# Values by whole tiles, four input sums on TensorE, and last halves that read h in place, in a four-layer graph network

## The chip, the cores and the metric

The kernel runs on one core of a Trainium2 chip. A core has five engines that work side by side and wait for each other by semaphores: TensorE (PE in the profile; PEld is its weight load), VectorE (DVE), ScalarE (ACT), GpSimd (POOL) and SyncE (SP, which here only issues DMAs). TensorE reads SBUF and writes PSUM; DVE and ACT read both. The metric is the device time of one execution, in microseconds (us); the runs are summed up by their median. The profiled execution is one more run, and has its own time and its own span, from the first to the last instruction.

## The reference

`x` holds 128 graphs of 64 nodes with 256 features, all fp32. Four layers follow one another, and each adds its graph network to `x` and normalises over the features:

```python
x = _layernorm(x + _L0_gnn_ref(x, adj, ...), axis=-1)
x = _layernorm(x + _L1_gnn_ref(x, adj, adj, ...), axis=-1)
x = _layernorm(x + _L2_gnn_ref(x, adj, ...), axis=-1)
x = _layernorm(x + _L3_gnn_ref(x, adj, ...), axis=-1)
```

Layer 0 aggregates over the graph, applies a two-layer perceptron and normalises both of its stages over all 8192 rows (a batch norm). Layer 1 aggregates, then runs attention with four heads of 64 and a perceptron:

```python
q = (x1 @ Wq).reshape(B, N, H, hd).transpose(0, 2, 1, 3)
v = (x1 @ Wv).reshape(B, N, H, hd).transpose(0, 2, 1, 3)
attn = jax.nn.softmax(scores, axis=-1)
o = jnp.einsum('bhnm,bhmd->bhnd', attn, v)
```

Layer 2 is two graph convolutions and then four LSTMs (p = 1 to 4), each over windows of p nodes; the last state of a window replaces the node at its end. Layer 3 is one graph attention over `h @ W`, with scores from two vectors:

```python
Wh = jnp.einsum('bnf,fo->bno', h, W)
e = s1[:, :, None] + s2[:, None, :]
attention = jax.nn.softmax(e, axis=-1)
h_prime = jnp.einsum('bij,bjo->bio', attention, Wh)
```

## The kernel before

The 8192 rows are cut into 16 blocks of 512 rows: 8 graphs of 64 nodes, laid out as four tiles of 128 rows (two graphs one above the other) by 256 features. `tm` views a buffer of 128x1024 by rows (tile, feature), `fm` by features (two chunks of 128 features, 512 rows). PSUM is used as four buffers of 128x1024 (`PS`); SBUF has eight temporaries of that size and more that become free later (`mem`). All matmuls are fp32.

A recording layer writes the program out in full. Every piece of work is a generator that yields a `step`: the engine, its expected time, how many PSUM buffers (`ps`) and temporaries (`sl`) it takes or gives back, and for TensorE the way the array is divided (`tbl`: whole, "columns" for halves, "quarter"). `flow` (L144) is a planner: it keeps a clock for each engine, takes the step that can start soonest, and so fixes, when the program is built, the order of instructions on each engine. A margin added to the start time is multiplied by a number drawn from `DRAWS`, one seed for each 50 us of planned time, so other seeds give another order everywhere. Where the plan has TensorE idle for over about a microsecond, `keep_awake` (L136) puts filler matmuls of 512 columns (L142) whose result nobody reads.[...]

The places that the change touches:

- `end_block` (L767) ends layer 0 for a block. It loads the block's input (L771), applies the batch norm's scale and shift to H on ACT (L774), transposes it to rows by eight transposes on TensorE (`to_tm`, L376), and adds the input on DVE (L782). Blocks are ended in the order 0, 1, 12, 13, 14, 15, 2, 3 and so on, the first six of them around the first blocks of layer 1. `block` (L789) is layer 1; its layer norms are statistics on DVE (L302 to L304), a power on POOL (L325), one small DVE step (L328) and four ACT steps (L331).
- In `block`, queries and keys are made by `mm_fm` (L382), then the values (L846). The attention's last product needs a head's values on the same partitions as its attention weights, and heads lie in pairs on the two halves of 64 partitions. Before, values are computed in halves of the array: 32 matmuls of 64 output rows by 128 columns, which leaves both halves in place, so one ACT copy of 128x1024 (L856) empties the PSUM buffer.
- The LSTMs of layer 2 keep h transposed in `hT`: features on partitions, and in the free dimension chunk, node and graph, with 32 graphs of a quarter of the batch side by side. Their matmuls are L1113, L1185 and, for the last units of p = 4, L1321 and L1323; their last write of h in such a unit is L1446. `units_of` splits the last quarter's p = 4 in two units of 16 graphs (blocks 12 and 13, and 14 and 15).
- `last_block` (L1513) is layer 3 for a block, or for half of one (two tiles) in the last quarter of the batch, blocks 12 to 15. It loads the rows of `x` that layer 2 left in DRAM (L1518), copies h from `hT` into the order of graphs (ACT, L1524), transposes it (L376), adds half of it to `x` on DVE (L1535; h is kept doubled), normalises, transposes again (L370), copies to SBUF (L1549, L1551), multiplies with W and the score vectors (L1564), makes the scores (L1588, L1589), the softmax (L1593 to L1604), transposes it (L1610), applies it (L1620), adds (L1631), normalises and stores (L1635).

Of the kernel before, what the change touches and what calls it, by code (L numbers as in the profile page):

```python
# [11 lines left out]
ALU = mybir.AluOpType  # L12
# [3 lines left out]
P = 128  # L16
B, N, D = 128, 64, 256
NBLK = 16
TB = 512
NT = 4  # L20
# [8 lines left out]
LAG, LAG_T = 0.06, 0.2  # L29
MARGIN = {"T": 0.5, "V": 0.5, "S": 0.5}  # L30
STRETCH = 50.0
DRAWS = [119, 456, 684, 0, 152, 590, 97, 0, 0, 316, 775, 750, 291, 668, 396, 690, 972, 316, 700, 299, 810, 345, 289, 861, 902, 463, 567, 883, 455, 277, 848, 910, 108, 288, 531, 607, 103, 756, 415, 205, 829, 978, 419, 437, 870, 596, 976, 248, 270, 919]


@with_exitstack
def kernel(ctx: ExitStack, tc: tile.TileContext, a: dict, out: bass.AP):
    nc = tc.nc
    V, S, G, T = nc.vector, nc.scalar, nc.gpsimd, nc.tensor
# [11 lines left out]
    def tm(s):  # L50

        return s.rearrange("p (t d) -> p t d", t=NT)
# [64 lines left out]
    def mark(*key):  # L117
        done[key] = Clock.end
# [7 lines left out]
    def step(e, us, ps=0, sl=0, waits=True, at=None, tbl=None):  # L126

        return (e, us, ps, sl, waits, at, tbl)
# [113 lines left out]
    Xs = [Xp[i // 2][:, i % 2, :] for i in range(NBLK)]  # L248
# [3 lines left out]
    H = [fm(s) for s in Hs]  # L252
    hT = [t.rearrange("p (c n b) -> p c n b", c=2, n=N) for t in Hg]
    XD = [dram.tile([P, NT, D], F32, tag=f"xd{i}", name=f"xd{i}") for i in range(NBLK)]

    PS = Stock([ctile([P, NT * D], f"ps{j}", psp) for j in range(4)])
    mem = Stock([ctile([P, NT * D], f"t{j}", big) for j in range(TEMPS)])
# [15 lines left out]
    halves = slice(0, N), slice(N, P)  # L273
    for s in range(2):
        h = halves[s]
# [8 lines left out]
    ident = ctile([P, P], "ident")  # L284
# [34 lines left out]
    def ln_steps_act(y):  # L319

        n = y.shape[1]
        yield step("V", 0.3 + 0.53 * n)
        mv, rs = stats(y)
        yield step("G", 1.0)
        G.tensor_tensor(rs, rs, neghalf[:, :n], ALU.pow)  # L325
        yield step("V", 0.2, tbl="m")
        nm = sm.tile([P, n], F32, tag="ln_nm", name="ln_nm")
        V.scalar_tensor_tensor(nm, mv[:, :, 0], -1.0, rs, ALU.mult, ALU.mult)  # L328
        yield step("S", 0.1 + 0.5 * n)
        for t in range(n):  # L330
            S.activation(  # L331
                y[:, t, :], y[:, t, :], AF.Identity, scale=rs[:, t : t + 1], bias=nm[:, t : t + 1]
            )
# [38 lines left out]
    def to_tm(ps, yT):  # L372

        for t in range(ps.shape[1]):
            for c in range(2):
                T.transpose(ps[:, t, c * P : (c + 1) * P], yT[:, c, t * P : (t + 1) * P], ident)  # L376
# [13 lines left out]
    def mm_tm(ps, yT, w, nk):  # L390

        for t in range(NT):
            for k in range(nk):
                T.matmul(
                    ps[:, t, :],
                    yT[:, k, t * P : (t + 1) * P],
                    w[:, k, :],
                    start=(k == 0),
                    stop=(k == nk - 1),
                )  # L400
# [22 lines left out]
    with c0:  # L423
# [310 lines left out]
        Wc, Wq, Wk, Wv = (WA[:, j, :].rearrange("p (k m) -> p k m", k=2) for j in range(4))  # L734
# [24 lines left out]
    sc2, sh2, _ = bn["bn2"]  # L759

    Wv_par = Wv.rearrange("p k (u r e) -> p k r u e", u=2, r=2)

    NORMED = range(1)

    def end_block(i):  # L767
        x = X[i]
        yield step("Q", 6.0, sl=1)
        xin = mem.take()  # L770
        nc.sync.dma_start(tm(mem[xin]), x_blk[i])  # L771
        for c in range(2):
            yield step("S", 0.7)
            S.activation(  # L774
                H[i][:, c, :], H[i][:, c, :], AF.Identity, scale=sc2[:, c : c + 1], bias=sh2[:, c : c + 1]
            )
        yield step("T", 0.9, ps=1)
        ps = PS.take()
        to_tm(tm(PS[ps]), H[i])
        mark("h", i)  # L780
        yield step("V", 1.25, ps=-1)
        V.tensor_tensor(x, tm(PS[ps]), tm(mem[xin]), ALU.add)  # L782
        PS.give(ps)
        mem.give(xin)
        if i in NORMED:
            yield from ln_steps_act(x)
        mark("end", i)

    def block(i):  # L789
        x = X[i]  # L790
# [4 lines left out]
        ps = PS.take()  # L795
# [6 lines left out]
        ps = PS.take()  # L802
# [14 lines left out]
        ps = PS.take()  # L817
        s_x1 = mem.take()
        to_fm(fm(PS[ps]), y)
        yield step("S", 1.05, ps=-1)  # L820
        x1T = fm(mem[s_x1])
# [3 lines left out]
        for w in (Wq, Wk):  # L825
            yield step("T", 3.45, ps=1, sl=1)
            ps = PS.take()
# [8 lines left out]
        qT, kT = fm(mem[qk[0]]), fm(mem[qk[1]])  # L836


        yield step("T", 3.6, ps=1, sl=1, tbl="columns")
        ps = PS.take()  # L840
        s_v = mem.take()
        pv = PS[ps].rearrange("p (b u e) -> p b u e", b=8, u=2)
        for b in range(8):
            for r in range(2):
                for k in range(2):
                    T.matmul(  # L846
                        pv[r * N : (r + 1) * N, b, :, :],
                        x1T[:, k, b * N : (b + 1) * N],
                        Wv_par[:, k, r, :, :],
                        start=(k == 0),  # L850
                        stop=(k == 1),
                    )
        mem.give(s_x1)
        yield step("S", 1.05, ps=-1, waits=False)
        v = mem[s_v].rearrange("p (b u e) -> p b u e", b=8, u=2)
        S.copy(mem[s_v], PS[ps])  # L856
        PS.give(ps)

        yield step("G", 2.4, waits=False, tbl="m")
# [4 lines left out]
        ps = PS.take()  # L864
        s_e = mem.take()
        pq = PS[ps].rearrange("p (r g m) -> p r g m", r=2, g=8)
        for t in range(NT):
            for u in range(2):
                for s in range(2):
                    b = 2 * t + s  # L870
                    for r in range(2):
# [4 lines left out]
                            start=True,  # L876
                            stop=True,
# [4 lines left out]
        e = mem[s_e].rearrange("p (g r m) -> p g r m", g=8, r=2)  # L882
# [19 lines left out]
        ps = PS.take()  # L902
# [9 lines left out]
        ps = PS.take()  # L912
        s_o = mem.take()
        po = fm(PS[ps])
        for b in range(8):
            t, s = b // 2, b % 2
            for u in range(2):
                for r in range(2):
# [4 lines left out]
                        start=True,  # L923
                        stop=True,
# [7 lines left out]
        ps = PS.take()  # L932
# [9 lines left out]
        ps = PS.take()  # L942
# [13 lines left out]
        for hf in range(2):  # L956
            yield step("T", 3.45, ps=1, sl=1)
            ps = PS.take()
# [14 lines left out]
        ps = PS.take()  # L973
        for t in range(NT):
            for k in range(4):
# [4 lines left out]
                    start=(k == 0),  # L980
                    stop=(k == 3),
# [82 lines left out]
    def hT_block(i):  # L1064

        return hT[i // 4][:, :, :, (i % 4) * 8 : (i % 4) * 8 + 8]
# [443 lines left out]
        return None if ("ws", p) not in done else max(t, done[("ws", p)])  # L1510


    def last_block(i, t0=0, nt=NT):  # L1513

        yield step("Q", 4.0, sl=1)
        s_x = mem.take()
        x = tm(mem[s_x])[:, :nt, :]
        nc.sync.dma_start(x, XD[i][:, t0 : t0 + nt, :])  # L1518
        r = nt / NT
        yield step("S", 0.2 + 1.9 * r, sl=1)  # L1520
        s_h = mem.take()
# [7 lines left out]
        ps = PS.take()  # L1529
        px = tm(PS[ps])[:, :nt, :]  # L1530
# [5 lines left out]
        PS.give(ps)  # L1536
        yield from ln_steps_act(x)

        yield step("T", 0.9 * r, ps=1, sl=1)
        ps = PS.take()  # L1540
        s_xT = mem.take()
        px = fm(PS[ps])[:, :, : nt * P]
# [11 lines left out]
        for t in range(0, nt, 2):  # L1554
            end = t == nt - 2
            yield step("T", 1.75, ps=1, sl=int(t == 0))
            ps = PS.take()
# [4 lines left out]
            for j in range(2):  # L1562
                for k in range(2):
# [4 lines left out]
                        start=(k == 0),  # L1568
                        stop=(k == 1),
# [13 lines left out]
        e, aT, d = (mem[s_e][:, j * nt * N : (j + 1) * nt * N].rearrange("p (t m) -> p t m", t=nt) for j in range(3))  # L1583
        G.tensor_tensor(d, bc_mid(unit2, nt), bc_last(s12[:, :nt, 1], N), ALU.mult)
        yield step("T", 0.1 + 0.9 * r, ps=1)
        ps = PS.take()
# [19 lines left out]
        ps = PS.take()  # L1606
# [8 lines left out]
        ps = PS.take()  # L1615
        po = PS[ps].rearrange("p (e u d) -> p e u d", e=2, u=2)
        for t in range(0, nt, 2):
            for j in range(2):
                for h in range(2):
# [4 lines left out]
                        start=True,  # L1624
                        stop=True,
# [17 lines left out]
    for i in blocks:  # L1643
        while n < at_end.get(i, NBLK):
            j = ends[n]
# [27 lines left out]
    for g in range(NG - 1):  # L1673
        read = [("read", i) for i in range(4 * g, 4 * g + 4)]
# [53 lines left out]
    def last_of(i, *part):  # L1728
# [17 lines left out]
        start=done["bn2", 0],  # L1746
# [49 lines left out]
```

## Time and profile before

| | |
|---|---|
| median of 3 runs | 2317.06 us (2316.89 to 2318.54) |
| the profiled execution | 2318.26 us, its span 2316.5 us |
| granted TensorE clock, mean | 0.997 |
| TensorE waits by the profile, all over | under 2 us each but for one of 5.5 near the start |
| filler matmuls (L142) | 29 (58 records): 24.9 us, at 0.43 us a record |
| last matmul to the end | 10.1 us |

The page gives the busy time of each engine and its share of the span, then the span in 40 slices with one digit a slice for each engine (9 is 90% or more). The view by stages gives the same in microseconds between two limits, with the granted clock and DMA at its end. The timeline lists instructions of one line together: start, time from the first start to the last end, engine, line, operation, what it writes and reads, shapes, how many records, and in brackets the idle time before it and who ended it. A matmul's end is modelled, so records overlap. The view of one line gives shortest, median and longest duration in nanoseconds for each name it writes and reads.

### The profile page before, as it was taken

To read this page: it belongs to the slowest core of one execution; us is meant where nothing else is said; L and a number is where in the kernel's file an instruction comes from. 1 tells how busy PE (TensorE), PEld (TensorE's weight loads), DVE (VectorE), ACT (ScalarE), POOL (GpSimd) and SP (SyncE) were. 2 spreads that over 40 slices of the span, in tenths; PEclk is the share of its full clock that TensorE was granted. 3 is DMA by queue.
4 is the path that set the end of the run, shared out by engine and by line. 5 is a ranking of instruction groups with operands and counts; after the bars stand their busy time and mean duration, and the time that the engine had idled before them with its cause. 6 is when DMAs were issued, how large, how long until landed. Compare 5 with 4: busy or idle time off the path is not lost. (4 is left out here: it accounts for less than half of the span.)

```text
span 2316.5 us, 40592 instructions
## 1 busy us (share of the span) xinstructions
PE 2270.1 (98%) x16974; PEld 1757.4 (76%) x16974; DVE 1332.9 (58%) x2869; ACT 1176.1 (51%) x2265; POOL 437.1 (19%) x323
## 2 busy tenths in 40 slices
PE   8999999999999999999999999999999999999997
PEld 5558667666666767567667888999999889888884
DVE  5557776767565668437444444454445655664577
ACT  2257556555554545544544343444434644654576
POOL 0012133232322235113220001001100110111012
PEclk9999999999999999999999999999999999999999
DMA  6100411000000000000100000000001000001111
GB/s 173 47 1 1 138 38 33 10 11 10 10 10 10 11 10 19 28 2 28 37 28 19 1 1 1 19 1 1 1 1 37 1 10 28 19 19 37 37 56 55
DMA packets 42632, 57.90 MB, mean 25 GB/s; under 512 B 6224, under 2 KB 35536, under 8 KB 42448
## 3 DMA queue, kind: packets, MB, share of 16 engines
q1 hardware_dynamic: 41344, 54.22, 7.1%
q8 instruction: 133, 2.18, 0.4%
q10 hardware_dynamic: 1104, 1.08, 0.1%
q14 instruction: 51, 0.42, 0.1%
HBM read 38.52 MB, written 16.78 MB: 24 GB/s over the span
## 5 line engine op out<-in xcount | busy, mean ns | idle before, releaser
L325 POOL TENSOR_TENSOR ln_rs<-ln_rs,neghalf 128x4 f32<-128x4 f32 (+1 forms) x104 | 111.8, 1075 | 722.5 <-DVE ln_rs L304 573.0
L1185 PE MATMUL ps<-x,x 128*128 128x256 f32 x832 | 204.5, 379 | 0.0
L1185 PE MATMUL ps<-t,x 128*128 128x256 f32 x736 | 179.0, 380 | 0.8 <-DVE t L1244 0.8
L1081 ACT ACTIVATE x<-ps,bih 128x512 f32<-128x512 f32 (+5 forms) x185 | 95.5, 552 | 150.4 <-PE ps L1113 97.7
L1185 PEld LDWEIGHTS ps<-x,x 128*128 128x128 f32 x832 | 156.0, 190 | 18.7
L1185 PEld LDWEIGHTS ps<-t,x 128*128 128x128 f32 x736 | 138.2, 190 | 20.3 <-DVE t L1244 1.2
L1081 ACT ACTIVATE t<-ps,bih 128x512 f32<-128x512 f32 (+5 forms) x151 | 79.5, 563 | 127.2 <-PE ps L1113 85.0
L331 ACT ACTIVATE x<-x,ln_nm,ln_rs 128x256 f32<-128x256 f32 x212 | 110.2, 593 | 43.8 <-DVE ln_nm L328 43.3
L382 PE MATMUL ps<-t,W1T 128*128 128x512 f32 x256 | 115.3, 595 | 0.0
L1081 ACT ACTIVATE x<-x,bih 128x512 f32<-128x512 f32 (+5 forms) x142 | 72.1, 559 | 44.2 <-DVE x L1251 44.2
L303 DVE BATCH_NORM_AGGREGATE ln_mv<-ln_st 128x2 f32<-128x6 f32 x448 | 81.6, 182 | 15.3
L302 DVE BATCH_NORM_STATS2 ln_st<-x 128x6 f32<-128x256 f32 x224 | 89.7, 401 | 0.3
L1113 PE MATMUL ps<-h,wL 128*128 128x192 f32 (+2 forms) x456 | 89.7, 351 | 0.0
L1113 PE MATMUL ps<-h,x 128*128 128x256 f32 x384 | 86.8, 380 | 0.0
L1113 PE MATMUL ps<-t,wL 128*128 128x512 f32 x192 | 83.9, 593 | 1.2 <-ACT t L909 1.2
L1113 PEld LDWEIGHTS ps<-h,wL 128*128 128x128 f32 x456 | 70.0, 190 | 17.4 <-issue 16.7
L382 PEld LDWEIGHTS ps<-t,W1T 128*128 128x128 f32 x256 | 46.4, 190 | 47.5 <-issue 47.3
L1113 PEld LDWEIGHTS ps<-h,x 128*128 128x128 f32 x384 | 72.8, 190 | 10.4 <-issue 0.5
L1244 DVE COPY x<-ps 128x256 f32<-128x256 f32 (+2 forms) x71 | 26.7, 377 | 86.6 <-PE ps L1185 86.2
L1251 DVE TENSOR_TENSOR x<-ps,x 128x512 f32<-128x512 f32 (+2 forms) x71 | 42.4, 598 | 51.0 <-PE ps L1185 41.0
L331 ACT ACTIVATE t<-t,ln_nm,ln_rs 128x256 f32<-128x256 f32 x104 | 54.1, 592 | 32.1 <-DVE ln_nm L328 32.1
L1113 PEld LDWEIGHTS ps<-t,wL 128*128 128x128 f32 x192 | 36.3, 190 | 44.7 <-issue 42.8
(715 smaller groups left out, 5408.6 us busy)
## 6 DMA issues: line engine op xcount, KB each, us to landing
t<-in_x_dram SPq DMA_DIRECT2D x24, 512.0 KB, 5.5
xd<-x SPq DMA_DIRECT2D x16, 512.0 KB, 2.7
h<-in_x_dram SPq DMA_DIRECT2D x7, 512.0 KB, 4.0
x<-xd SPq DMA_DIRECT2D x6, 512.0 KB, 3.4
out_dram<-x SPq DMA_DIRECT2D x6, 512.0 KB, 2.9
wL<-in_L_gnn_Wih_dram SPq DMA_DIRECT2D x2, 1024.0 KB, 5.0
x<-in_L_gnn_Whh_dram SPq DMA_DIRECT2D x2, 1024.0 KB, 5.2
t<-xd SPq DMA_DIRECT2D x4, 512.0 KB, 4.3
```

Source lines behind the costliest of these rows:

```text
L302: V.bn_stats(st[:, t, :], y[:, t, :])
L303: V.bn_aggr(mv[:, t, :], st[:, t, :])
L325: G.tensor_tensor(rs, rs, neghalf[:, :n], ALU.pow)
L331: S.activation(y[:, t, :], y[:, t, :], AF.Identity, scale=rs[:, t : t + 1], bias=nm[:, t : t + 1])
L382: T.matmul(ps[:, c, :], w[:, k, (off + c) * P : (off + c + 1) * P], yT[:, k, :], start=(k == 0), stop=(k == nk - 1),)
L1081: S.activation(dst, z, AF.Tanh, bias=bl[:, p - 1, 2 * g + c : 2 * g + c + 1], scale=(1.0 if g == 2 else 0.5) * (1.0 if p == 1 else 0.5),)
L1113: T.matmul(spread(fm(PS[ps])[:, j, :n], q), WL[p][0][:, k, m], x_of(0, q)[:, k], start=(k == 0), stop=(k == 1),)
L1185: T.matmul(dst, WS[p][name](k, g), y[:, k], start=first and k == 0, stop=k == 1, skip_group_check=not first)
L1244: V.tensor_copy(y[:, 1, :], v[:, 0, :])
L1251: V.tensor_tensor(y[:, 0:2, :], v[:, 2:4, :], y[:, 0:2, :], ALU.add)
```

## The change

There are three edits and new seeds.

Values are computed by `mm_tm` like the other products: eight matmuls of 128 rows by 256 columns. The pairs of heads then lie in the free dimension, and four ACT copies of 64 partitions by 512 elements bring each half of the rows to the half of the partitions where its head belongs.

For blocks 12 to 15 (`SUM_BY_T`), `end_block` no longer transposes and adds. TensorE multiplies the identity with the input's tile (256 columns, starts the sum) and H's two chunks with the identity (128 columns each, added on top), four times, and ACT copies the sum to SBUF. These are ordinary matmuls, not transposes.

In `last_block`, half blocks read h where it lies: for each tile, graph and chunk one matmul has h of that graph (64 columns, 32 numbers apart) as its stationary operand and the identity as its moving one, in halves of the array. DVE adds the result in two instructions. Whole blocks go on as before, in `sum_of_copies`.

```diff
-DRAWS = [119, 456, 684, 0, 152, 590, ...]
+DRAWS = [555, 824, 612, 0, 95, 823, ...]
...
+    SUM_BY_T = (12,13,14,15)
...
-        yield step("T", 0.9, ps=1)
+        yield step("T", 2.65 if i in SUM_BY_T else 0.9, ps=1)
         ps = PS.take()
-        to_tm(tm(PS[ps]), H[i])
-        mark("h", i)
-        yield step("V", 1.25, ps=-1)
-        V.tensor_tensor(x, tm(PS[ps]), tm(mem[xin]), ALU.add)
+        if i in SUM_BY_T:
+            for t in range(NT):
+                T.matmul(tm(PS[ps])[:, t, :], ident, tm(mem[xin])[:, t, :], start=True, stop=True)
+                for c in range(2):
+                    T.matmul(
+                        tm(PS[ps])[:, t, c * P : (c + 1) * P],
+                        H[i][:, c, t * P : (t + 1) * P],
+                        ident,
+                        start=False,
+                        stop=True,
+                        skip_group_check=True,
+                    )
+            mark("h", i)
+            yield step("S", 1.05, ps=-1)
+            S.copy(Xs[i], PS[ps])
+        else:
+            to_tm(tm(PS[ps]), H[i])
...
-        yield step("T", 3.6, ps=1, sl=1, tbl="columns")
+        yield step("T", 3.45, ps=1, sl=1)
         ps = PS.take()
         s_v = mem.take()
-        pv = PS[ps].rearrange("p (b u e) -> p b u e", b=8, u=2)
-        for b in range(8):
-            for r in range(2):
-                for k in range(2):
-                    T.matmul(
-                        pv[r * N : (r + 1) * N, b, :, :],
-                        x1T[:, k, b * N : (b + 1) * N],
-                        Wv_par[:, k, r, :, :],
...
-        yield step("S", 1.05, ps=-1, waits=False)
-        S.copy(mem[s_v], PS[ps])
+        mm_tm(tm(PS[ps]), x1T, Wv, 2)
+        mem.give(s_x1)
+        pv = PS[ps].rearrange("p (t u r e) -> p t u r e", t=NT, u=2, r=2)
+        v = mem[s_v].rearrange("p (b u e) -> p b u e", b=8, u=2)
+        yield step("S", 2.4, ps=-1, waits=False)
+        for s in range(2):
             for r in range(2):
+                S.copy(v[halves[r], s::2, :, :], pv[halves[s], :, :, r, :])
...
+    def direct_sum(i, t0, nt, x):
+
+        r = nt / NT
+        yield step("T", 1.8 * r, ps=1, tbl="columns")
+        ps = PS.take()
+        px = PS[ps].rearrange("p (e u d) -> p e u d", e=2, u=2)
+        for t in range(nt):
+            for s in range(2):
+                for c in range(2):
+                    T.matmul(
+                        px[halves[s], t % 2, t // 2, c * P : (c + 1) * P],
+                        hT_block(i)[:, c, :, 2 * (t0 + t) + s],
+                        ident,
+                        start=True,
+                        stop=True,
+                    )
+        mark("read", i)
+        yield step("V", 0.1 + 1.2 * r, ps=-1)
+        for j in range(2):
+            V.scalar_tensor_tensor(x[:, j::2, :], px[:, j, : nt // 2, :], 0.5, x[:, j::2, :], ALU.mult, ALU.add)
...
+        if nt < NT:
+            yield from direct_sum(i, t0, nt, x)
+        else:
+            yield from sum_of_copies(i, t0, nt, x)
```

More of the change, by code (lines that the diff above doesn't have):

```diff
@@ L31 @@
 STRETCH = 50.0
-DRAWS = [119, 456, 684, 0, 152, 590, 97, 0, 0, 316, 775, 750, 291, 668, 396, 690, 972, 316, 700, 299, 810, 345, 289, 861, 902, 463, 567, 883, 455, 277, 848, 910, 108, 288, 531, 607, 103, 756, 415, 205, 829, 978, 419, 437, 870, 596, 976, 248, 270, 919]
+DRAWS = [555, 824, 612, 0, 95, 823, 924, 783, 0, 77, 0, 664, 0, 363, 656, 902, 351, 574, 489, 0, 99, 684, 176, 923, 880, 530, 427, 46, 867, 911, 330, 952, 468, 0, 995, 634, 175, 950, 362, 0, 989, 997, 384, 358, 116, 975, 487, 599, 389, 118]
 @with_exitstack
@@ L759 @@
     sc2, sh2, _ = bn["bn2"]
-    Wv_par = Wv.rearrange("p k (u r e) -> p k r u e", u=2, r=2)
     NORMED = range(1)
+    SUM_BY_T = (12,13,14,15)
     def end_block(i):
@@ L776, in end_block @@
             )
-        yield step("T", 0.9, ps=1)
+        yield step("T", 2.65 if i in SUM_BY_T else 0.9, ps=1)
         ps = PS.take()
-        to_tm(tm(PS[ps]), H[i])
-        mark("h", i)
-        yield step("V", 1.25, ps=-1)
-        V.tensor_tensor(x, tm(PS[ps]), tm(mem[xin]), ALU.add)
+        if i in SUM_BY_T:
[15 more added lines that the diff above has]
+            to_tm(tm(PS[ps]), H[i])
+            mark("h", i)
+            yield step("V", 1.25, ps=-1)
+            V.tensor_tensor(x, tm(PS[ps]), tm(mem[xin]), ALU.add)
         PS.give(ps)
@@ L836, in block @@
         qT, kT = fm(mem[qk[0]]), fm(mem[qk[1]])
-        yield step("T", 3.6, ps=1, sl=1, tbl="columns")
+        yield step("T", 3.45, ps=1, sl=1)
         ps = PS.take()
         s_v = mem.take()
-        pv = PS[ps].rearrange("p (b u e) -> p b u e", b=8, u=2)
-        for b in range(8):
-            for r in range(2):
-                for k in range(2):
-                    T.matmul(
-                        pv[r * N : (r + 1) * N, b, :, :],
-                        x1T[:, k, b * N : (b + 1) * N],
-                        Wv_par[:, k, r, :, :],
[L850 to L853, printed above, removed]
-        yield step("S", 1.05, ps=-1, waits=False)
-        v = mem[s_v].rearrange("p (b u e) -> p b u e", b=8, u=2)
-        S.copy(mem[s_v], PS[ps])
+        mm_tm(tm(PS[ps]), x1T, Wv, 2)
[4 more added lines that the diff above has]
+        for s in range(2):
+            for r in range(2):
+                S.copy(v[halves[r], s::2, :, :], pv[halves[s], :, :, r, :])
         PS.give(ps)
@@ L1510, in sums_at, with sum_of_copies @@
         return None if ("ws", p) not in done else max(t, done[("ws", p)])
[L1513 to L1518, printed above, removed]
+    def sum_of_copies(i, t0, nt, x):
         r = nt / NT
@@ L1537, in last_block @@
         yield from ln_steps_act(x)
+    def direct_sum(i, t0, nt, x):
[17 more added lines that the diff above has]
+            V.scalar_tensor_tensor(x[:, j::2, :], px[:, j, : nt // 2, :], 0.5, x[:, j::2, :], ALU.mult, ALU.add)
+        PS.give(ps)
+        yield from ln_steps_act(x)
+    def last_block(i, t0=0, nt=NT):
+        yield step("Q", 4.0, sl=1)
+        s_x = mem.take()
+        x = tm(mem[s_x])[:, :nt, :]
+        nc.sync.dma_start(x, XD[i][:, t0 : t0 + nt, :])
+        r = nt / NT
+        if nt < NT:
+            yield from direct_sum(i, t0, nt, x)
+        else:
+            yield from sum_of_copies(i, t0, nt, x)
         yield step("T", 0.9 * r, ps=1, sl=1)
```

## The prediction, made before the changed kernel ran

> **What bounds the kernel.** I read the busy shares first, then the 40 slices, then the timeline of TensorE where its slices aren't full, and last the stages around the end.
>
> ```profile
> PE 2270.1 (98%) x16974; PEld 1757.4 (76%) x16974; DVE 1332.9 (58%) x2869; ACT 1176.1 (51%) x2265; POOL 437.1 (19%) x323
> PE   8999999999999999999999999999999999999997
> ...
> 300.00:500.00 200.00, 196.63 (x1928) 137.78 (x1926) 130.50 (x269) 111.85 (x162) 64.94 (x38) 1.00 0.07 24
> 2261.00:2316.50 55.50, 39.44 (x304) 26.43 (x302) 40.98 (x154) 36.31 (x105) 11.87 (x17) 0.90 0.17 58
> ```
>
> The last two lines are stages: their limits, their length, then busy time of PE, PEld, DVE, ACT and POOL. TensorE (PE) carries the span: nothing else is over 60%, and only the first and the last slices show room. So I count TensorE's work up to the last product of the LSTM (L1323, ending at 2261), and beyond it a tail of 55.5 us that hangs on latency (clock 0.90 there). Busy time must not be summed: it contains the pipeline's end of each matmul. I take start to start:
>
> ```profile
> 294.00 0.61 PE L1029 MATMUL ps<-bdAT,h 128*128 128x128 f32 x4
> ...
> 311.70 3.40 PE L394 MATMUL ps<-wA,t 128*128 128x256 f32 x15
> 314.94 1.04 PE L905 MATMUL ps<-ident,t 128*128 128x128 f32 x8
> 315.91 3.76 PE L846 MATMUL ps<-wA,t 128*64 128x128 f32 x64
> 319.60 1.16 PE L919 MATMUL ps<-h,t 64*64 64x64 f32 x64
> ```
>
> L394: (3.40 - 0.379)/14 = 0.216 us a record of 256 columns. L905: (1.04 - 0.273)/7 = 0.110 of 128 columns. L846: (3.76 - 0.273)/63 = 0.0553 of 128 columns in half the array. A transpose makes one record (L905: 8 for 8), an ordinary fp32 matmul two (L1029: 4 for 2). Entering the half-array form costs 315.91 - 314.94 - 8 x 0.110 = 0.09, leaving it 319.60 - 315.91 - 64 x 0.0553 = 0.15.
>
> **Values (16 blocks).** Out: 64 records x 0.0553 = 3.54. In: 16 x 0.216 = 3.46. That is -0.08 a block, -1.4 in all. The trace shows what a change of tiling costs, 0.09 and 0.15; the Trainium skill, "TensorEngine Tiling (Array Packing)", section Tiling Modes, says that such a change drains the array, without a time. By the rule, priced from the rows, every Values step saves two drains, 16 x 0.24 = 3.8. But the order of the built program decides: quarter-array neighbours remain, and all changes of form, priced one by one (0.09 into a narrower one, 0.14 to 0.15 out), go from 25.8 to 24.8: -1.0. I take that. Here the evacuation becomes four copies of 64x512 on ACT for one of 1.01. Nearest row: L1549, 128x512 out of PSUM, 0.58; four are 2.0 (overlapped) to 2.3, so +1.2 a block, +19.7 on ACT over 300 to 1150, where it is 53% busy (451 of 850 us). The buffer of PSUM is held that much longer; below nothing it can't go. Queued behind it on ACT are other blocks' copies. Cost taken: 0; the price if the cover fails is the slower rival below.
>
> **Four sums by TensorE (blocks 12 to 15).** Out: 8 transposes, 0.88, and a DVE addition of 1.22. In: 4 x 2 x 0.216 = 1.73 for the input and 8 x 2 x 0.110 = 1.76 for h, as these are no transposes: 3.49, so +2.6 each, +10.4 on TensorE; DVE loses 4.9, ACT gets four copies of 1.01. The matmuls now wait for the input's load instead of DVE. In the trace each of the first eight loads lands by 256.4 and TensorE comes to them after 258, so no stall; queued behind would be all of TensorE. The place has room:
>
> ```profile
> 250.14 7.03 PE L142 MATMUL ps<-ident 128*128 128x512 f32 x16
> 257.00 2.02 PE L376 MATMUL ps<-ident,h 128*128 128x128 f32 x17
> 259.52 1.86 PE L376 MATMUL ps<-ident,h 128*128 128x128 f32 x15 [0.50 <-ACT h L774]
> 261.21 5.32 PE L142 MATMUL ps<-ident 128*128 128x512 f32 x12
> 266.46 1.62 PE L358 MATMUL ps<-LnT,x 64*64 64x64 f32 x64
> 268.01 1.13 PE L142 MATMUL ps<-ident 128*128 128x512 f32 x2
> ...
> 280.96 2.74 PE L142 MATMUL ps<-ident 128*128 128x512 f32 x6
> 284.44 1.06 PE L370 MATMUL ps<-ident,t 128*128 128x128 f32 x8 [0.74 <-DVE t L814]
> ```
>
> L142 is filler: a record of 512 columns is (7.03 - 0.592)/15 = 0.43, a filler matmul 0.86, and 19 of them (16.3 us) lie between 250 and 286.6, where block 0's queries begin. There the changed order has 11, so 8 x 0.86 = 6.9 of filler goes and 10.4 of work comes: +3.5. Stalls of 0.50, 0.74, 0.24 and short ones go, some 1.6, since TensorE is now what is late: block 0's queries begin at about 288.5, +1.9. In all, filler falls from 29 to 22 matmuls, -6.0; four of those left stand in the middle of layer 1, seven fewer lie here and in the tail.
>
> **Last halves (eight, blocks 12 to 15).** Out of each: two ACT copies of 0.63, four transposes (0.44), one DVE sum of 0.68. In: 8 half-array matmuls x 2 x 0.0553 = 0.89, +0.45 each, +3.6; DVE two sums of 256, 0.75 by the like pair of L1631, +0.07. Blocks 0 to 11 keep their copies. The new stationary is h with a step of 32 numbers, which no matmul of the trace reads. The nearest row is the removed copy, which walks the same way:
>
> ```profile
> 2264.84 0.58 ACT L1549 COPY x<-ps 128x512 f32<-128x512 f32 x1 [0.33 <-PE ps L370]
> ...
> L1524 ACT COPY x<-h x14: 637/1092/1159, 1792.6 to 2274.3; 128x512 f32<-128x512 f32 x12, 128x256 f32<-128x256 f32 x2
> ```
>
> The first is a copy without steps, 0.58; the second the stepped one, median 1.09 (mostly of 512 elements): double. The Trainium skill, "SBUF — State Buffer", section Door 1: The DMA port swizzle, speaks against the change: fp32 reads that leave a 16-byte line each time pay. If weight loads pay that wholly, a half costs 1.78 and eight cost 7.1 more; if the load hides behind the running matmul, nothing. I take 1, since a 64-column load lies beside two records of another half; both ends are kept.
>
> **Sum up to the LSTM's last product.** Every matmul of both orders at these prices: before 2152.3 of work + 18.9 filler + 23.9 changes of form = 2195.1; after 2155.0 + 15.5 + 22.8 = 2193.3, because 9.9 us of earlier blocks' leftovers now come later. So -1.9, stalls -1.6, stepped reads +0.5 (those of blocks 12 and 13): **-3.0 at this point**.
>
> **The tail.**
>
> ```profile
> 2269.31 3.60 PE L142 MATMUL ps<-ident 128*128 128x512 f32 x8
> 2273.38 0.33 PE L376 MATMUL ps<-ident,t 128*128 128x128 f32 x1 [0.48 <-ACT t L1524]
> ...
> 2272.70 1.15 ACT L1524 COPY t<-h 128x256 f32<-128x256 f32 x2
> ```
>
> h is ready at 2267.1 (last write, L1446), but ACT gets to the copies at 2272.7, and TensorE idles or fills until 2273.4, 12.2 after the last product; the fourth half's sum starts at 2280.6. In the changed order 11.5 us of matmuls stand between the last product and the four direct groups, which then take 3.6 plus 0.5 for steps and need no ACT: the halves start 0.6 to 4 earlier, on average 2. Against that, one more block's attention (about 5 us on DVE, 4 on ACT, by the rows of a block) lies in the tail, where DVE is busy 41 of 55.5. I take **-2.0**, bounds -5 and +3.
>
> Sum: -3.0 - 2.0 = -5.0. The profiled execution took 2318.26 around a span of 2316.5: it becomes 2313.3. It lies 1.2 above the median of 2317.06, so I forecast **2312.1**. A measurement of this kernel tells about 0.2%, 4.6 us, from no change, and the forecast stands on that edge.
>
> **Rivals.**
> - *Hidden anyway* (chance 0.09): the halves of the tail are held by DVE and by the extra block, so the tail grows by 2 to 3 and the sum is -0.5: 2316.6. For it: DVE's share of the tail. Against: the copies did end the wait.
> - *Stalls in the body fall too* (0.16): 16 us of idle matmul time lie scattered in 300 to 2250 in waits under 2 us each; a new order could halve them, -8: 2304. For it: nothing but the reshuffling, which could as well add; against: the four fillers in layer 1 mark a gap that is new.
> - *Slower: ACT holds PSUM in layer 1* (0.23). Four buffers feed TensorE; Values' buffer is given back 1.2 later, 16 times, 19.7 in all. If ACT has more than about three buffers' worth of products (3 x 3.5 us) queued, TensorE waits for it; if 12 of the 19.7 show, the sum is +7: 2324. For it: TensorE did wait 1.4 on Values' copy once (L370 on L856); against: ACT has 45% free there, and that was the only time.
> - That the change doesn't do what it says is excluded by the order; copies of blocks 0 to 11 stay by design.
>
> **Chances.** Forecast 0.52, own range 2308 to 2316.5; 0.34 of it lies below 2312.4, 0.16 within, 0.02 above. With the rivals: faster 0.34 + 0.16 = 0.50, within 0.16 + 0.09 = 0.25, slower 0.25. The range of 2303 to 2325 takes in the rivals' times and both ends of the stepped reads.
>
> **What would show it.** L394's form in place of L846 in 3.5 us, ACT's four copies in 2.0 to 2.3 without TensorE waiting for them; the direct sums at 3.5 us each with block 0's queries at about 288.5; the LSTM's last product ending near 2258; direct groups of a half in 0.9 (1.8 would be stepped reads at full price); a tail of 53 to 54. Waits for ACT in 300 to 1150 of over 10 us, or a tail over 58, would make it wrong.

## The result: slower by 7.9 us, and the profile after

The changed kernel took 2324.85 us (median of 10 runs, 2321.61 to 2326.88) against 2316.93 for the kernel before on the same chip (10 runs, 2315.24 to 2319.98): ratio 1.0031, 95% interval 1.0023 to 1.0039. That is 12.7 us above the forecast and at the upper edge of the range. The profiled execution took 2322.76, its span is 2321.0.

First the page of the changed kernel, busy shares and TensorE's 40 slices:

```profile
PE 2273.9 (98%) x16352; PEld 1759.7 (76%) x16352; DVE 1340.3 (58%) x2873; ACT 1189.8 (51%) x2299; POOL 435.1 (19%) x323
...
PE   8999999999999999999999999999999999999997
```

At this scale nothing has moved: the shares are those of before to the per cent. So I cut the span at three instructions that both kernels have and compare the starts: the last product of layer 0, the first query product of block 0, and the LSTM's last product (L1323 before, L1333 after).

| stage, us | before | after | difference |
|---|---|---|---|
| start to layer 0's last product | 249.7 | 252.2 | +2.5 |
| to block 0's queries | 36.9 | 38.9 | +2.0 |
| to the LSTM's last product | 1974.1 | 1968.7 | -5.4 |
| tail, to the end of the span | 55.8 | 61.1 | +5.4 |
| span | 2316.5 | 2321.0 | +4.5 |

The medians differ by 7.9, not by 4.5. The granted clock shows most of the reason. In the profiled execution of before it fell to one half for 3.41 us twice; the stages view of these two pieces (limits, length, busy time of PE, PEld, DVE, ACT and POOL, granted clock, DMA share, GB/s):

```profile
796.29:799.70 3.41, 3.41 (x9) 2.71 (x10) 0.00 (x0) 2.09 (x4) 1.16 (x1) 0.53 0.00 0
2294.74:2298.15 3.41, 3.31 (x16) 2.62 (x16) 2.25 (x11) 1.17 (x4) 0.70 (x1) 0.53 0.15 46
```

Half of 3.41 is lost: 1.7 us in the third stage, and in the tail 1.6 (a group of eight L1564 took 3.47 there, 1.91 elsewhere). The profiled execution of after has no such window before its last matmul. Without them the third stage is -3.7 and the tail +7.0, and the four add up to +7.8. That is near the difference of the medians, though the executions behind these hold windows of their own, which weren't counted. The tail is firmer. All four profiles of the old order in the experiments below (e9 to e12), which have no window in the tail, give 54.1 to 54.2, and three of the changed order (e2 to e4) give 61.1, as the changed kernel does. So +7.0 is measured, and it goes with the order and not with the edits: e12 has all three edits, and its tail is 54.2.

Now the tail. The stages view from the last product to the end, of the changed kernel and then of before:

```profile
2259.86:2321.00 61.14, 45.35 (x403) 33.98 (x401) 45.35 (x173) 36.53 (x119) 13.07 (x19) 0.91 0.16 53
```

```profile
2260.74:2316.50 55.76, 39.70 (x305) 26.62 (x303) 40.98 (x154) 36.57 (x105) 11.87 (x17) 0.90 0.17 57
```

PE is busy 5.7 longer, DVE 4.4, and ACT no less although it lost eight copies: one more whole block's attention runs here (W's product on whole blocks has 40 records in the tail where before had 16). The timeline of TensorE in the changed kernel shows what lies ahead of the last halves:

```profile
2259.45 1.03 PE L1333 MATMUL ps<-t,x 128*128 128x256 f32 x4
2260.31 0.59 PE L1628 MATMUL ps<-x,bdones 128*128 128x256 f32 x2
2260.74 0.59 PE L1629 MATMUL ps<-s,ident 128*128 128x256 f32 x2
2261.17 1.91 PE L1604 MATMUL ps<-Wx,x 128*128 128x258 f32 x8
2262.92 1.03 PE L370 MATMUL ps<-ident,x 128*128 128x128 f32 x8
2263.79 1.04 PE L370 MATMUL ps<-ident,h 128*128 128x128 f32 x8
...
2266.23 2.01 PE L1604 MATMUL ps<-Wx,x 128*128 128x258 f32 x8
2268.17 1.09 PE L1660 MATMUL ps<-h,x 64*64 64x256 f32 x16
2269.20 2.01 PE L1604 MATMUL ps<-Wx,h 128*128 128x258 f32 x8
2271.05 1.90 PE L1604 MATMUL ps<-Wx,x 128*128 128x258 f32 x8
2272.88 4.40 PE L1554 MATMUL ps<-ident,h 128*64 128x128 f32 x64
```

No filler is left here and TensorE never idles, yet the four direct groups (L1554, 64 records) start 13.0 us after the last product (2259.86); before, the transposes started 12.6 after it (2273.38 and 2260.74). And DVE, in its timeline, takes the four halves up at nearly the same instants as before (2274.49, 2276.54, 2277.14 and 2280.56 there):

```profile
2274.35 0.76 DVE L1564 SCALAR_TENSOR_TENSOR x<-ps,x 128x256 f32<-128x256 f32 x2 [0.71 <-ACT t L1616]
2276.30 0.76 DVE L1564 SCALAR_TENSOR_TENSOR t<-ps,t 128x256 f32<-128x256 f32 x2
2276.97 0.74 DVE L1564 SCALAR_TENSOR_TENSOR h<-ps,h 128x256 f32<-128x256 f32 x2
2280.28 0.76 DVE L1564 SCALAR_TENSOR_TENSOR x<-ps,x 128x256 f32<-128x256 f32 x2
```

The fourth half comes 0.3 earlier, and the end is 4.5 later: 40.7 us follow it where 35.9 did, 34.3 without the window. Counted from the last product, the fourth half comes at 20.4 us where before had 19.8. So 0.6 of the 7.0 lies ahead of it and 6.4 behind it. The chain of waits of the changed kernel runs almost wholly along TensorE until 2291. Behind that it runs mainly along DVE, with 3.5 us of TensorE from 2295.6:

```profile
2286.98 3.86 PE ps L1604 x16
2290.84 0.44 PE ps L370 x4
2291.27 0.22 PE ps L1628 x2
2291.50 0.24 PE ps L1629 x2
2291.76 0.30 DVE h L1633
2292.09 0.30 DVE h L1635
```

### The profile page after: what moved, and what is told of

The parts are those of the page before. It is cut to its first block, busy times and chain, and to the rows that moved or that the text cites. A ratio compares the mean times of both kernels' runs of the same rounds, so it can differ in the third digit from the quotient of the medians.

```text
span 2321.0 us, 39405 instructions
## 1 busy us (share of the span) xinstructions
PE 2273.9 (98%) x16352; PEld 1759.7 (76%) x16352; DVE 1340.3 (58%) x2873; ACT 1189.8 (51%) x2299; POOL 435.1 (19%) x323
## 4 chain that ended last, share of the span: by engine, by line
PE 93%; DVE 4%; ACT 2%; issue 1%; DMA 0%; ACTq 0%; POOL 0%; DVEq 0%
PE ps L1195 27%; PE ps L382 16%; PE ps L1123 15%; PE ps L394 9%; PE ps L986 4%; PE ps L659 4%; PE ps L358 3%; PE ps L1604 2%; PE ps L1331 2%; PE ps L1333 2%; PE ps L370 2%; PE ps L376 1%; PE ps L929 1%; PE ps L882 1%; DVE ln_st L302 1%
## 5 line engine op out<-in xcount | busy, mean ns | idle before, releaser
L1195 PE MATMUL ps<-x,x 128*128 128x256 f32 x928 | 225.3, 379 | 0.3 <-DVE x L1263 0.3
L1195 PEld LDWEIGHTS ps<-x,x 128*128 128x128 f32 x928 | 173.6, 190 | 22.4 <-issue 1.0
L1091 ACT ACTIVATE t<-ps,bih 128x512 f32<-128x512 f32 (+5 forms) x179 | 93.0, 556 | 140.4 <-PE ps L1123 92.1
L1091 ACT ACTIVATE x<-ps,bih 128x512 f32<-128x512 f32 (+5 forms) x163 | 86.0, 561 | 143.5 <-PE ps L1123 107.0
L1195 PE MATMUL ps<-t,x 128*128 128x256 f32 x608 | 150.0, 380 | 0.0
L1195 PEld LDWEIGHTS ps<-t,x 128*128 128x128 f32 x608 | 114.1, 190 | 15.5 <-issue 0.9
L1091 ACT ACTIVATE t<-t,bih 128x512 f32<-128x512 f32 (+2 forms) x118 | 59.1, 551 | 54.4 <-DVE t L1261 53.3
L1091 ACT ACTIVATE x<-x,bih 128x256 f32<-128x256 f32 (+5 forms) x130 | 66.6, 565 | 30.7 <-DVE x L1261 30.6
L1123 PEld LDWEIGHTS ps<-h,x 128*128 128x128 f32 x384 | 72.7, 190 | 10.4 <-ACT t L1383 0.5
L1123 PE MATMUL ps<-x,wL 128*128 128x512 f32 x168 | 73.3, 593 | 1.2 <-ACT x L1420 1.2
```

What stands on the lines that cost most here:

```text
L1091: S.activation(dst, z, AF.Tanh, bias=bl[:, p - 1, 2 * g + c : 2 * g + c + 1], scale=(1.0 if g == 2 else 0.5) * (1.0 if p == 1 else 0.5),)
L1123: T.matmul(spread(fm(PS[ps])[:, j, :n], q), WL[p][0][:, k, m], x_of(0, q)[:, k], start=(k == 0), stop=(k == 1),)
L1195: T.matmul(dst, WS[p][name](k, g), y[:, k], start=first and k == 0, stop=k == 1, skip_group_check=not first)
```

## The experiments

Fifteen kernels ran. In all of them a difference is against runs of the kernel before on the same chip (medians of 2316.2 to 2316.9 us), where the changed kernel, in its own comparison, stands at +7.9. In most of them the order of instructions is held fixed, by keeping the planner's steps as they were and changing only what a step emits; so an edit's effect can be seen without a new order around it.

### Order or edits (e1 to e4)

e1 is the changed kernel planned with the seeds of before:

```diff
-DRAWS = [555, 824, 612, 0, 95, ...]
+DRAWS = [119, 456, 684, 0, 152, ...]
```

> The changed kernel with the seeds of before: all three edits, another order from the start of layer 1. Theory 'paid' (TensorE's added work is on the path wherever TensorE has no idle time, and filler is path too): by the prices of the prediction its list holds 2243.7 us up to the end (29.3 of it filler) where before holds 2227.7 and the changed one 2233.3, so 10 to 16 us over before. Theory 'tail' (the refitted order of the end is the loss, the edits are a gain): only 7.8 us of matmuls stand ahead of the last halves instead of 11.5, so -1 to +3. Theory 'ACT' (four copies for Values hold PSUM): as the changed kernel, +8.

Measured: 2352.01 us, +35.3, ratio 1.0148 (1.0134 to 1.0162). Every expectation missed: the edits under seeds that weren't fitted to them (chosen for this kernel's own steps) are far worse. The last product starts 17.6 later than in the changed kernel and the tail is 11 longer. So seeds can't be exchanged to isolate the edits.

e2 takes the old seeds for layer 0 alone, and pins the planner's state behind it, so that all that follows keeps the changed kernel's order:

```diff
-            d = DRAWS[j] if j < len(DRAWS) else 0
+            ds = DRAWS_0 if start == 0.0 else DRAWS
+            d = ds[j] if j < len(ds) else 0
```

> The changed kernel with the old seeds in layer 0 alone; from there on the order of every engine is that of the changed kernel. Theory 'paid': the order of layer 0 costs 2.5 (its last product starts 252.2 instead of 249.7), and nothing later takes it up, as TensorE is the bound: +5.4 over before, last product of layer 0 at 249.7. Theory 'tail' and 'ACT': layer 0 doesn't matter much, later waits take it up: +7 to +8.

Measured: 2320.97, +4.3, ratio 1.0018 (1.0012 to 1.0025), 3.6 less than the changed kernel. Layer 0 up to its last product, where no edit lies, had been ordered anew as well. Over the profiles of all runs its last product starts at 248.9 to 250.8 in the old order and 251.0 to 253.4 in the new one. The means, of seven and of ten profiles, are 2.3 apart. So about 2.3 us of the 3.6 are layer 0's order; in e2's own profile the product starts 2.2 earlier than in the changed kernel's. The rest of the 3.6 isn't explained.

e3 puts the transposes and the DVE addition back in place of the four sums, e4 the half-array values with their one copy, both in the changed kernel's order:

```diff
-        mm_tm(tm(PS[ps]), x1T, Wv, 2)
+        for b in range(8):
+            for r in range(2):
+                for k in range(2):
+                    T.matmul(pv[r * N : (r + 1) * N, b, :, :], ...)
...
+        S.copy(mem[s_v], PS[ps])
```

> The changed kernel with the order kept, but blocks 12 to 15 transposed and added on DVE as before: TensorE loses 10.4 us of work around block 0's first steps, DVE gets four additions there. Theory 'paid': TensorE was late there by 2 to 4, then block 0's chain takes over: first query product near 288 instead of 290.9, +4 to +6 over before. 'ACT': ACT loses four copies, hardly any change, +7.5. If the sums were a gain (DVE was what bounds): over +10.

> The changed kernel with the order kept, but Values in halves of the array with one copy of 1.01 us as before. Theory 'paid': TensorE gets 1.4 of work and 2.9 of changes of form, priced list 2237.6 for 2233.3: +4 on the changed kernel, +11 to +12 over before. Theory 'ACT' (PSUM held 19.7 us longer in all): 8 to 12 less than the changed kernel, -4 to 0 over before. 'tail': no change, +8.

Measured: e3 2324.15, +7.5, ratio 1.003 (1.0017 to 1.0042): TensorE lost 10.4 us of work there and the median stayed. That doesn't make the sums free. The timeline of TensorE in e3 shows waits where the sums had been, and the changed kernel has none over 0.4 us there:

```profile
266.49 2.49 PE L358 MATMUL ps<-LnT,x 64*64 64x64 f32 x64 [2.49 <-ACT x L331]
...
287.00 1.09 PE L370 MATMUL ps<-ident,t 128*128 128x128 f32 x8 [3.22 <-DVE x L782]
```

Behind the first of them the clock fell to one half at 268.4 (the group took 2.49 us for the 1.16 of L358 in the changed kernel), and once more at 1094.4. Without these two windows e3's span of 2321.8 would be 2318.4, 2.6 less than the changed kernel's. That is an estimate from one profile, but none of e3's six executions has a mean clock over 0.997, so its median holds windows too. On an undisturbed clock the sums cost some 2.6 us.

e4 2327.54, +10.9, ratio 1.0043 (1.003 to 1.0056): in this order undoing the Values edit costs near 3 us by the medians. It costs 4.4 by the spans of the two profiles, neither of which has a window (2325.4 and 2321.0); the expectation from TensorE's list was 4. The theory that its four copies hold PSUM falls. The trace of the changed kernel agrees. The view of one line (shortest, median, longest in ns) has the copies at 0.58, four in 2.3, and nearly nobody waits for them in 16 blocks:

```profile
L866 ACT COPY t<-ps x36: 562/580/584, 303.5 to 1085.5; 64x512 f32<-64x512 f32 x36
...
who waited for it (us, times):
  ACT t L1091: 1.1, 1
  PEld ps L929: 0.8, 1
  PEld ps L358: 0.3, 1
```

### What moves the tail (e5, e6)

Both are the changed kernel with other seeds for the last 120 us only; the order up to 2190 us is the same.

```diff
-DRAWS = [..., 116, 975, 487, 599, 389, 118]
+DRAWS = [..., 354, 694, 780, 976, 0, 427]
```

> The changed kernel, with an order that differs only in the last 120 us: 11.8 us more of the earlier blocks' matmuls come ahead of the LSTM's last product, 5.4 instead of 11.5 us of matmuls lie between that product and the last halves, and DVE's list behind its last write of h falls from 43.2 to 34.3 us at the same prices (the changed kernel's trace has 40.4 us busy there, so 32.1 here). Theory A (the tail is about 13 us of waits plus DVE's list): last product at 2271 to 2272, from the last write of h to the end 44 to 46 instead of 53.4, in all 2 to 4 longer than the changed kernel, +10 to +12 against before. Theory B (the halves are late because of the matmuls ahead of them): the tail falls by 6, +13 to +15. Theory C (the tail is latency, whatever lies in it): tail 53, +19.

> The changed kernel, with an order that differs only in the last 120 us the other way: 5.2 us fewer matmuls ahead of the LSTM's last product, only 4.6 us between it and the last halves, and 53.6 instead of 43.2 us on DVE's list behind its last write of h (50 at the trace's level). Theory A (waits of 13 plus DVE's list): last product near 2254.5, from the last write of h to the end 61 to 64 instead of 53.4, in all 3 to 6 longer than the changed kernel, +11 to +14 against before. Theory B (matmuls ahead of the halves): the tail falls by 7, in all 12 shorter than the changed kernel, -4 against before. Theory C (latency alone): 5 shorter than the changed kernel, +3.

Measured: e5 2333.75 (+17.5, ratio 1.0077, 1.0062 to 1.0092), e6 2333.58 (+17.3, ratio 1.0076, 1.0061 to 1.0091). From the last write of h to the end the profiles have 50.8, 53.4 and 71.4 us for few, the changed kernel's and many leftovers; DVE is busy 31.3, 40.4 and 51.1 of it. Theory B falls by e6: with the matmuls ahead of the halves down from 11.5 to 4.6 us by the list, this stretch grew by 18 (the whole tail by 16). But e6 didn't free the halves. Filler and waits stand there in the matmuls' place, and the direct groups start 12.2 us after the last product, where the changed kernel has 13.0 and e5 12.5. Theory A has the direction right and the size wrong: the time in which DVE isn't busy is 13 in the two fitted orders (before: 36.1 busy of 49.4, 11.7 idle without the window) and about 20 in these two. Leftovers cost their place. The seven us more go with orders that weren't fitted; what in them costs it isn't shown.

### The direct reading (e7, e8, e10)

e7 gives the last halves their copies and transposes back, in the changed kernel's order. e8 only takes the step out of the reads:

```diff
-    hT_block(i)[:, c, :, 2 * (t0 + t) + s],
+    hT[i // 4].rearrange("p c n b -> p c (n b)")[:, c, first : first + 64],
```

> The changed kernel in its own order, but the eight last halves are again two ACT copies and four transposes each, in temporaries that lie free, with one DVE addition. TensorE's list is 4.7 us shorter, half of it ahead of the last product. If the direct groups cost what they hold of TensorE and spared nothing: last product 2.4 earlier, tail 0 to 1 shorter because DVE sets it, in all +4.5 to +6 against before instead of +7.9. If the copies are worth sparing (ACT is late in the tail): the tail's sums come 1 to 3 later and the whole stays at +7 to +11.

> The changed kernel in its own order, but the direct groups of the last halves read 64 numbers that lie side by side as their stationary operand instead of 64 that lie 32 apart; they are h of other nodes and graphs, so the result of layer 3 is another one for blocks 12 to 15. If the steps are what makes a record 0.065 instead of 0.055 us: a group of a half 0.89 instead of 1.04, weight load 137 instead of 219 ns, eight groups 1.2 shorter, last product 0.6 earlier, +7 against before. If the records are longer for another reason (64 columns into half the array): 1.04 again, +7.9.

Measured: e7 2328.03 (+11.8, ratio 1.0051, 1.0036 to 1.0066), slower than the changed kernel although TensorE's list is 4.7 shorter. The waits of TensorE in e7 from 2180 to 2262 (us in all, times, longest) show what takes the place; the changed kernel has no such wait there:

```profile
PE ps L376 <- ACT t L1553: 2.8, 4, 2.2
PE ps L376 <- ACT h L1553: 1.5, 4, 0.9
```

Behind the wait of 2.2 us the clock fell to one half, at 2199.8. Without this window e7's span of 2323.8 is 1.1 us over the changed kernel's. The mean clock of its four executions goes from 0.998 down to 0.995, so a part of the 3.9 by which the medians differ is windows.

e8: 2321.14 (+4.9, ratio 1.002, 1.0011 to 1.0029). The view of L1554, in the changed kernel and then in e8:

```profile
L1554 PEld LDWEIGHTS ps<-ident,h x128: 188/219/237, 2185.2 to 2276.9; 128*64 128x64 f32 x128
```

```profile
L1554 PEld LDWEIGHTS ps<-ident,h x128: 132/137/138, 2185.1 to 2275.2; 128*64 128x64 f32 x128
```

The steps are what makes the load longer, 219 ns for 137. The last product starts 1.05 earlier in e8 and the tail is 0.6 shorter, 1.7 together by profiles without a half-clock window. The medians give 3, since the changed kernel's median lies among its longer executions (mean clock 0.997). The executions with a mean clock of 0.998 average 2322.3 in the changed kernel and 2320.3 in e8, about 2 apart.

e10 is the other way round: the kernel before in its old order, with the direct reading alone. It was run with e9, e11 and e12, next.

### Each edit in the old order (e9 to e12)

The kernel before, every instruction in its old place. e9 has Values alone, e10 the last halves alone, e11 both, e12 all three edits, with eight of the filler matmuls between 250 and 286 left out for the sums.

```diff
+LEFT_OUT = (11, 12, 13, 14, 15, 16, 18, 19)
...
+            if Clock.filler - 1 in LEFT_OUT:
+                continue
             T.matmul(fm(PS[j])[:, 0, :], ident, bc_mid(ident, 4), start=True, stop=True)
```

> The kernel before, every instruction in its old place, with the Values edit alone: eight matmuls of 256 columns for 32 of half the array, four ACT copies for one. TensorE's list is 1.4 of work and 2.95 of changes of form shorter (2227.7 to 2223.3). Theory (the edit is a gain wherever it stands, as undoing it in the changed order cost about 3): -2.5 to -4.4 against before. Rival (four copies hold the buffer of PSUM, in an order that was not fitted for them): 0 to +7.

> The kernel before in its old order, with the direct reading of h by the last halves alone (no ACT copy, eight half-array matmuls of 1.04 us a half for four transposes of 0.44). TensorE's list is 4.7 longer by the unstepped price, 6.1 with the steps; 3.3 of it ahead of the last product. Theory 1 (a cost of TensorE that is paid ahead of the last product, and in the tail DVE keeps its pace): +2 to +3.5. Theory 2 (sparing the copies is worth more than it costs, as undoing it in the changed order made that slower): -1 to -3.

> The kernel before in its old order, with Values and the last halves changed, the sums as they were. If the two edits don't touch each other: the sum of the two single runs. By the list +0.3 to +1.7 against before; by theory 2 of the halves -4 to -6.

> All three edits in the order of the kernel before, with eight of its filler matmuls left out where the four sums come (6.9 us for 10.4 of work). If the three edits are harmless and the order is what made the changed kernel slower: +1 to +4 against before, 4 to 7 below the changed kernel. If the edits themselves cost the time: +7 to +9 as in the changed kernel.

| kernel | median us | against before | ratio (95%) |
|---|---|---|---|
| e9 Values | 2315.02 | -1.9 | 0.9995 (0.9987 to 1.0003) |
| e10 halves | 2319.99 | +3.1 | 1.0015 (1.0008 to 1.0022) |
| e11 both | 2319.12 | +2.2 | 1.0012 (1.0005 to 1.0018) |
| e12 all | 2326.18 | +9.3 | 1.0042 (1.0028 to 1.0055) |

For Values the profiles say less than the medians: e9's span, without a window, is 2313.0, and that of before without its two windows 2313.2. So Values gives 4.4 in the order fitted to it and 0.2 to 1.9 in the old one.

The direct reading costs 3.1, as theory 1 had it. Its tail is that of the same order with copies: the stages view, e9 (copies) and then e10 (direct), from the last product to the end:

```profile
2258.86:2313.00 54.14, 38.09 (x305) 25.42 (x303) 40.95 (x154) 36.45 (x105) 11.87 (x17) 0.93 0.18 59
```

```profile
2264.10:2318.30 54.20, 39.98 (x353) 28.28 (x352) 41.15 (x158) 32.49 (x97) 11.87 (x17) 0.93 0.18 59
```

ACT does 4.0 less and TensorE 1.9 more, and the tail stays to 0.1. That e7 found the copies worse and e10 the direct groups worse is no contradiction: each puts an edit into an order that was fitted for the other form. In e7 the misfit shows as waits and a window; in e10 the 3.3 us that the list has more ahead of the last product are enough.

The sums cost 7.1 from e11 to e12, for 3.5 more on TensorE's list. The timeline of TensorE in e12 shows two waits; e11 has none at the first of these places (0.5 ahead of an earlier transpose) and 0.7 at the second:

```profile
268.83 2.72 PE L363 MATMUL ps<-LnT,x 64*64 64x64 f32 x64 [1.60 <-ACT x L336]
...
294.06 1.68 PE L375 MATMUL ps<-ident,t 128*128 128x128 f32 x8 [2.45 <-DVE t L836]
```

ACT's copies of the sums stand ahead of block 0's layer norm (L336) in its list and themselves wait 8.1 us in all for the sums. Behind each of the two waits the clock fell to one half, at 270.5 and 294.4, which costs up to 1.7 us each in this profile. In its own order the changed kernel has these waits away, and its queries are 2.0 late.

So the same three edits are +9.3 in the old order and +7.9 in the fitted one: fitting won back little. Values alone is the best of the kernels tried, but its interval takes in no change; it isn't shown to be faster than before.

### Whose work sets the tail (e13 to e15)

The changed kernel in its order; behind the last product the whole blocks do less on TensorE, less on DVE, or both.

```diff
-                for k in range(2):
+                nk = 1 if nt == NT and Clock.pairs == PAIRS else 2
+                for k in range(nk):
...
-        mv, rs = stats(y)
+        one = n == NT and Clock.pairs == PAIRS
+        n = 1 if one else n
+        mv, rs = stats(y[:, :n])
```

> The changed kernel in its own order, but behind the LSTM's last product the whole blocks multiply with only the first half of W's 256 input features (their layer 3 is another function): 20 records of 0.22 us fewer, 4.4 us, 3.5 of it ahead of the direct groups. If TensorE sets the tail: from the last product to the end 60.9 - 3.5 to 4.4 = 56.5 to 57.4. If DVE sets it: 60 to 60.9.

> The changed kernel in its own order, but behind the LSTM's last product the layer norm of a whole block takes mean and variance from the first of its four tiles for all four (another function for these blocks): four layer norms with 3 x 0.53 us less on DVE each, 6.4 in all, 1.6 ahead of the first direct sum and 4.8 behind it. If DVE sets the tail: from the last product to the end 54.5 to 57. If TensorE sets it: 60 to 60.9.

> Both of the former. If one engine sets the tail alone, this equals the run without that engine's share; if the two follow one another (TensorE up to the last halves, DVE behind them), the gains add up to 8 to 10: 51 to 53.

The stages view of the three, from the last product to the end:

```profile
2261.54:2320.60 59.06, 41.29 (x383) 30.45 (x381) 44.99 (x173) 36.56 (x119) 13.09 (x19) 0.93 0.16 55
```

```profile
2261.07:2320.40 59.33, 45.30 (x403) 33.95 (x401) 39.55 (x149) 36.34 (x119) 11.38 (x19) 0.92 0.16 54
```

```profile
2262.84:2319.20 56.36, 40.85 (x383) 30.23 (x381) 39.27 (x149) 36.47 (x119) 11.34 (x19) 0.92 0.17 57
```

With 4.1 less on TensorE the tail falls by 2.1, with 5.8 less on DVE by 1.8, with both by 4.8, more than the two together. The medians are 2322.24, 2322.13 and 2319.04 (+5.7, +5.6 and +2.5; ratios 1.0026, 1.0022 and 1.0009, the last from 1.0001 to 1.0018). None of the expectations was met: no engine sets the tail alone, and they don't simply follow one another either, for then the sum would have been 8 to 10. Each takes over a good part of what the other gives up.

## Why the prediction was wrong

By its own steps, with the half-clock windows of before taken out:

- **Prices and instructions** held. Values' eight matmuls take 3.5 us, the four copies 2.3, a direct sum 3.5 to 3.7 for 3.49, a direct group of a half 1.04, where 0.89 was no cost for the steps and 1.78 their full price. For the steps of all eight I took 1; e8 gives 1.7 by the profiles.
- **Block 0's queries +1.9**: +2.0 from layer 0's end.
- **-3.0 at the LSTM's last product**: it became +0.8. Of the gap, 2.5 is layer 0, which I never priced, since no edit lies in it; the new seeds order it anew all the same, and e2 gives 3.6 back by taking its old order, 2.2 of it by the profiles at this point. The rest is 1.3, for which no run names a cause.
- **The tail, -2.0 with bounds -5 and +3**: this step failed. It was +7.0. It had two parts. *"The halves start 0.6 to 4 earlier, on average 2"*: they didn't. The matmuls in front of them, 11.5 us by the list, take 12.6 in the trace (2260.31 to 2272.88) and fill the time that ACT's copies had taken. DVE, busy without a gap from 2276.2, takes the fourth half up in its own order at 2280.3. From the last product to this half's sum it is 0.6 us longer than before, not 2 shorter. That fewer matmuls in front would have helped isn't shown: e6 had filler there instead. e10 shows the direct groups to be worth nothing, to 0.1 us, in a tail with nothing else changed. *"One more block's attention lies in the tail"*: I counted the 9.9 us of matmuls that left the stretch ahead of the last product as a gain there, and let the idle time of the tail take them in for nothing. It doesn't: idle time of a tail lies between steps that wait for each other. Behind the fourth half's sum the tail grew by 6.4 us. Behind the last write of h, DVE's busy time grew by 4.3 and the tail by 4.0 as profiled, 5.6 without the window. e13 to e15 take about as much work out of the tail as it had gained, though from all its whole blocks and not from the extra one alone: 20 of the 24 records of W's product that it has more than before, and 5.8 us of DVE where 4.4 had come. With both gone, 4.8 of the 7.0 go, so the tail answers to this work on both engines; 2.2 stay (56.4 for 54.1 to 54.2).
- Forecast -5.0. Put right: -3.0 + 3.8 + 7.0 = +7.8.

Among the rivals, "hidden anyway" had the mechanism (DVE and the extra block hold the tail), at 2 to 3 us of it instead of 7. "ACT holds PSUM" had the size, 2324, by a mechanism that isn't there: e4 and the view of L866. "Stalls in the body fall too" isn't seen: the third stage fell by 3.7, and the forecast without this rival had 4.9 there (-3.0 less the +1.9 ahead of it). A tail of over 58 was named as what would make the forecast wrong.

What stays open: how much of the 7.0 is the extra block and how much the place it was given; e15 leaves 2.2 for the place and whatever else the order changed. e5, with fewer leftovers in the tail, shortened it by 2.1 and lost 13 ahead of it, but in an order that wasn't fitted.

## What to carry to other kernels

Work that an order moves from a full stretch into a latency-bound tail isn't free there: price it in the tail by the engines that it visits, and take idle time as cover only where nothing in it waits for the moved work's engines. When a change brings a new order, compare it at milestones, including stages without an edit, before summing the edits. To price one edit, hold the order fixed; but do it both ways, since an edit can be worth 4.4 us in the order fitted to it and next to nothing in another, as Values was. Where differences are of a few us, count the half-clock windows in each profile before explaining a difference of medians.

## What the runs showed of the hardware

- The granted clock fell to one half for 3.41 us at a time, with TensorE 98% busy over the span. The seventeen profiles hold 14 such windows ahead of the last matmul, none to three in each. Thirteen of them begin during a wait of TensorE of 1.6 to 3.5 us or within 2 us of its end (1.81 us ahead of 796 in the kernel before); only the one at 2295, with waits of 0.94 and 0.57 ahead of it, doesn't. The wait doesn't decide alone: of 21 waits of 1.6 us or more between 15 and 2300 us, 8 brought no window, one of 3.22 among them. The changed kernel has a wait of 2.11 us near 970 (L882) that the old order hasn't; in nine profiles of the changed order it takes 1.8 to 2.4, and four of them have a window behind it.
- Each window costs up to 1.7 us. The changed kernel's ten runs lie in two groups, 2321.6 to 2322.8 (mean clock 0.998) and 2324.6 to 2326.9 (0.997), so one profile can differ from the median by the number of its windows. The groups' means are 3.3 apart, twice one window's cost; what else parts them isn't shown.
- By the profiles' clock records the full clock begins 10.9 to 14.5 us into the span, at 11.5 in the kernel before and at 13.0 in the changed one. A group of 128 small matmuls (L358) at 9 us took 3.10 us in the first and 3.69 in the second. So 0.9 of the changed kernel's +2.5 in layer 0 is there already when the first product with W1 starts (12.23 and 13.09); the means over the profiles, 2.3 apart, are the better figure for layer 0's order.
- A stationary operand of 64 columns, 128 bytes apart, loads in 219 ns instead of 137 (L1554, e8), and 64 records of this form take 4.40 us instead of 3.77 (the timelines of the changed kernel and of e8), 0.065 instead of 0.0555 a record. So of the 82 ns by which the load is longer, about 10 show in each record.
